# A half tile of 64 tokens paired on TensorE in a graph layer, and window values written to DRAM in 128-token tiles

## The chip, the cores and the metric

The kernel runs on one core of a Trainium2 chip. The metric is the device time of one execution in microseconds (us). TensorE is called PE, VectorE DVE, ScalarE ACT, GpSimd POOL; SP (SyncE) issues the DMAs.

## The reference

Four images of 56 x 56 positions (T = 3136 tokens) with 256 channels pass through four layers, all in fp32. Each layer adds its result to x, from a group norm of x:

- layer 0: attention of each token to its 7x7 neighbourhood, 8 heads;
- layer 1: a graph over all tokens of an image;
- layer 2: attention over neighbourhoods with dilation 1 and 2;
- layer 3: attention within shifted 7x7 windows of 49 tokens.

The change is in layers 1 and 3. Layer 1, cut to what matters:

```python
xn = x / norm(x, axis=-1)
A = exp(5.0 * (einsum('bnc,cc,bmc->bnm', xn, W_adj, xn) - max))
A = A * (1 - eye(n))
A = A / sum(A, -1)
diff = rowsum(A) * (x @ W_aff.T + b_aff) - (A @ x) @ W_aff.T
y = leaky_relu(layernorm(diff) * gamma + beta)
```

W_adj acts as a diagonal, so the matrix of exponentials is symmetric. Layer 3 is `softmax(q k^T * scale + bias + mask) v` for each window and head, followed by an output projection.

## The kernel before

**Layer 1** (L1331 to L1569). An image's tokens form NB = 25 tiles of 128, of which the last holds 64 tokens and is padded with zeros to 128. Chunks of four tiles are loaded by `tokens` (L1346): normalised, `xw` = x W_aff with a last column of -1 (257 columns), and `xnT`, the tokens at unit length with channels on the partitions. A block of exponentials is computed once for each pair of tiles j <= i and used for both, because the matrix is symmetric. The order of PE's work is that of a list of units (b, j, first, last): row tile j against up to four tiles from `first` to `last`. For each unit in turn:

- `transposed` (L1417) transposes its blocks, and ACT copies them to `at`;
- `logits` (L1404) of the *next* unit: two matmuls of up to 512 columns into `ps_s`, then ACT's exp into `e`; POOL clears the diagonal of a block with itself (L1414);
- `products` (L1429): for each tile i of the unit, `by_column` multiplies block e by xw of tile j into a PSUM bank `ps_v` (two banks, in turn), which DVE adds to `acc` of tile i (L1446; a copy for j = 0, L1444); `by_row` multiplies the transposed block by xw of tile i into `ps_o` of tile j (L1437).

When j has met all tiles, `finish` (L1465) forms and normalises its rows on DVE and POOL; its last step `add` (L1491 on) transposes the rows on PE (L1494) and adds them to x (L1502). Such small steps wait in a list and go out, when due, between the parts of a unit. `replace` (L1539) queues the chunks of the next image there as soon as the current image no longer needs their place, and `there` (L1533) runs what a unit's logits still lack.

**Values of layers 0 and 2.** `value_tiles` (L973) makes v = xn W_v in tiles of 128 tokens for a chunk of rows, in two pieces (a = 0, 1) of two tiles, adds the bias on DVE (L986), and after the second piece writes the whole to DRAM (`vd`, L991 and L993), from where it is gathered in the layout that attention needs (`vp`, L1688 in layer 2). A chunk's first tile begins with tokens left over from the chunk before (`left`, L969).

**Layer 3** (the code around L1837 to L1953). A row r is one of 32 rows of 8 windows, 392 tokens, handled as four window pairs of 98 tokens and in two halves of four heads (`hq`). `prepare` (L1859) normalises a row on DVE; `project_rows` (L1868) gives kT, qT and, by `value_rows` (L956), v for each window pair: 16 matmuls `ps_m<-w_wqkv,xn` with 98 rows of output and 256 columns (L962), evicted by DVE (L964). `quad` describes a half row for a shared attention routine: logits (L1025), exp and mask on ACT, DVE and POOL, products with v and with ones (L1040). The fill steps that PE does between logits and products are the output projection of row r-2 and the projections of row r+1 (L1929 to L1942). PE, DVE, ACT and POOL follow the written order in layer 3, PE does in layer 1; the rest, and SP's queue of DMAs throughout, is ordered by a scheduler at build time.

The functions that the change touches, with the line numbers of the profile:

Of the kernel before, what the change touches and what calls it, by code (L numbers as in the profile page):

```python
# [830 lines left out]
def direct_blocks(ctx: ExitStack, tc: tile.TileContext, d: dict, watch):  # L831
# [124 lines left out]
    def value_rows(v, a, n, xn, w, bias):  # L956

        pm = ps_m()
        for j in range(2):
            k = 2 * a + j  # L960
            for h in range(CC):
                nc.tensor.matmul(pm[:n, j * C:(j + 1) * C], lhsT=xn[:, h, k * n:(k + 1) * n],  # L962
                                 rhs=w[:, h, :], start=(h == 0), stop=(h == CC - 1))
        nc.vector.tensor_tensor(v[:, 2 * a:2 * a + 2, :], pm[:n, :].rearrange("p (j c) -> p j c", c=C),  # L964
                                bias[:n].rearrange("p (o c) -> p o c", o=1).to_broadcast([n, 2, C]), ALU.add)

# [6 lines left out]
    def value_tiles(v, a, c, n, xn, w, bias, dst):  # L973

        t0, t1 = c * n // P, (c + 1) * n // P if (c + 1) * n < T else -(-T // P)
        pm = ps_m()
        sizes = [min(P, T - t * P) for t in range(t0, t1)]
        mine = sizes[2 * a:2 * a + 2]
        for j, k in enumerate(mine):
            first = (2 * a + j) * P  # L980
            for h in range(CC):
                nc.tensor.matmul(pm[:k, j * C:(j + 1) * C], lhsT=xn[:, h, first:first + k], rhs=w[:, h, :],  # L982
                                 start=(h == 0), stop=(h == CC - 1))
        for k in sorted(set(mine)):
            js = [j for j, kj in enumerate(mine) if kj == k]
            nc.vector.tensor_tensor(  # L986
                v[:k, 2 * a + js[0]:2 * a + js[-1] + 1, :], pm[:k, js[0] * C:(js[-1] + 1) * C].rearrange("p (j c) -> p j c", c=C),
                bias[:k].rearrange("p (o c) -> p o c", o=1).to_broadcast([k, len(js), C]), ALU.add)
        if a == 1:
            whole = sizes.count(P)  # L990
            nc.sync.dma_start(out=dst[t0 * P:(t0 + whole) * P, :].rearrange("(k p) c -> p k c", p=P), in_=v[:, :whole, :])  # L991
            if whole < len(sizes):
                nc.sync.dma_start(out=dst[(t0 + whole) * P:T, :], in_=v[:sizes[-1], whole, :])  # L993
# [336 lines left out]

    def layer1(early, big, pool, brief):  # L1331
        NB = -(-T // P)
        real = lambda i: min(P, T - i * P)
# [4 lines left out]
        xnT = big.tile([P, CC, NB * P], FP, name="xnT")  # L1338
        xw = big.tile([P, NB, C + 1], FP, name="xw")
# [3 lines left out]
        nc.vector.memset(xw[T % P:, NB - 1, :], 0.0)  # L1343
        nc.vector.memset(xnT[:, :, T:], 0.0)

        def tokens(b, c, ps_a=ps_m):  # L1346

            tiles = range(4 * c, min(4 * c + 4, NB))
            n = sum(real(t) for t in tiles)
            k, m = real(tiles[0]), len(tiles)  # L1350
            box = {}

            def load():
                x = early.tile([P, CC, 512], FP, tag="x", name="x1")
                nc.sync.dma_start(out=x[:, :, :n], in_=tokens_of(1, b, 4 * c * P, n))
                x1 = box["x"] = early.tile([P, CC, 512], FP, tag="xn", name="xn1")
                sq = box["sq"] = early.tile([P, CC, 512], FP, tag="sq", name="sq", bufs=1)
                for h in range(CC):
                    normalise(x1[:, h, :n], x[:, h, :n], known(1, b), h)
                nc.scalar.activation(sq[:, :, :n], x1[:, :, :n], AF.Square)  # L1360
# [25 lines left out]
            def unit_length():  # L1386

                pm = ps_a()
                nc.tensor.matmul(pm[:, :n].rearrange("p (m k) -> p m k", k=k), lhsT=ones[:k, :], rhs=box["dg"][:k, :m, :k],
                                 start=True, stop=True)  # L1390
                nc.vector.tensor_tensor(xnT[:, :, 4 * c * P:4 * c * P + n], box["x"][:, :, :n],  # L1391
                                        pm[:, :n].rearrange("p (o k) -> p o k", o=1).to_broadcast([P, CC, n]), ALU.mult)

            return [load, lengths] + [lambda i=i: values(i) for i in range(0, m, 2)] + [unit_length]

        xd, out, xr = {}, {}, {}

# [6 lines left out]
        def logits(b, j, first, last):  # L1404

            n = (last - first) * P
            s = psum_tile("s", 2)
            for h in range(CC):
                nc.tensor.matmul(s[:, :n], lhsT=xd[j][:, h, :], rhs=xnT[:, h, first * P:last * P],  # L1409
                                 start=(h == 0), stop=(h == CC - 1))  # L1410
            e = pool.tile([P, 512], FP, tag="e", name="e1", bufs=3)
            nc.scalar.activation(e[:, :n], s[:, :n], AF.Exp, scale=5.0)  # L1412
            if first == j:
                nc.gpsimd.tensor_tensor(e[:, :P], e[:, :P], offd, ALU.mult)  # L1414
            return e

# [12 lines left out]
        def products(b, j, first, last, e, at):  # L1429
# [10 lines left out]
            def by_column(i):  # L1440
                pv = psum_tile("v", 2)
                nc.tensor.matmul(pv[:, :C + 1], lhsT=e[:, col(i)], rhs=xw[:, j, :], start=True, stop=True)  # L1442
                if j == 0:
                    nc.vector.tensor_copy(acc[:, i, :], pv[:, :C + 1])  # L1444
                else:
                    nc.vector.tensor_tensor(acc[:, i, :], acc[:, i, :], pv[:, :C + 1], ALU.add)  # L1446
# [10 lines left out]

        def residual(b, c):
# [6 lines left out]
        def finish(b, j):  # L1465

            n = real(j)
            y = pool.tile([P, C + 1], FP, tag="y", name="y", bufs=5)
# [3 lines left out]
            if j:  # L1472
                nc.vector.tensor_tensor(y[:n], out[j][:n, :C + 1], acc[:n, j, :], ALU.add)
            else:
                nc.vector.tensor_copy(y[:n], out[j][:n, :C + 1])
# [15 lines left out]
            def add():  # L1491
# [5 lines left out]
                while t0 < j * P + n:  # L1497
# [5 lines left out]
                    if t1 == (c + 1) * CH:  # L1503
# [7 lines left out]
        NC4 = -(-NB // 4)  # L1511
        units = [(b, j, i, min(i + 4, NB)) for b in range(NIMG) for j in range(NB) for i in range(j, NB, 4)]
        turn = iter(range(4 * NC4))
        fresh = [tokens(0, c, lambda: psum_tile(*(("v", 2), ("o", 2), ("t", 1), ("s", 2))[next(turn) % 4])) for c in range(NC4)]
        for c in range(2):
            fresh[c].pop(0)()
        for c in range(NC4):
            for step in fresh[c]:
                step()
            if c + 2 < NC4:  # L1520
                fresh[c + 2].pop(0)()
        scaled(0)
        e = logits(*units[0])
# [9 lines left out]
        def there(b, tile):  # L1533

            for item in [a for a in small if a[2] == (b, tile // 4)]:
# [3 lines left out]
        def replace(b, c):  # L1539
            load, *steps = tokens(b, c)  # L1540
            load()
            at = sum(a[2] is not None for a in small)
            small[at:at] = [(done + 8, step, (b, c)) for step in steps]

        for k, w in enumerate(units):
            b, j, first, last = w
            if first == j:
                residual(b, j * P // CH)
                residual(b, j * P // CH + 1)
                if b + 1 < NIMG and j % 4 == 2 and j >= 6:  # L1550
                    replace(b + 1, j // 4 - 1)
                if b + 1 < NIMG and j == NB - 1:
                    replace(b + 1, NC4 - 2)
                if b and j == 0:
                    replace(b, NC4 - 1)
            small_step()
            at = transposed(*w, e)
            if k + 2 < len(units) and units[k + 2][1] == units[k + 2][2]:
                scaled(units[k + 2][1])
            if k + 1 < len(units):  # L1560
                there(units[k + 1][0], units[k + 1][3] - 1)
                ahead = logits(*units[k + 1])
            small_step()
            products(*w, e, at)
            done += last - first
            if last == NB:
                small.append((done + 6, finish(b, j), None))
# [260 lines left out]
    def layer3(early, big, pool, brief):  # L1828
# [10 lines left out]
        xs, xns, qkv, attns = {}, {}, {}, {}  # L1839
# [19 lines left out]
        def prepare(r):  # L1859
# [3 lines left out]
            xn = xns[r] = early.tile([P, CC, WC], FP, tag="xn", name="xn3")  # L1863
            for h in range(CC):
                for w, xv in parts(xn[:, h, :], x[:, h, :]):
                    normalise(w, xv, known(3, r // 8), h)

        def project_rows(r):  # L1868
            xn = xns.pop(r)
            qT = pool.tile([P, CC, WC], FP, tag="q", name="q3")  # L1870
            kT = pool.tile([P, CC, WC], FP, tag="k", name="k3")
            v = pool.tile([98, 4, C], FP, tag="v", name="v3")
            qkv[r] = qT, kT, v
# [9 lines left out]
            def values(a):  # L1883
                value_rows(v, a, 98, xn, w_qkv[:, :, 2 * C:], bv3)

            return [lambda f=f, m=m: f(m) for m in range(2) for f in (keys, queries, values)]

        def quad(r, hq):
            b, wr = divmod(r, 8)
            qT, kT, v = qkv[r]  # L1890
# [14 lines left out]
            def piece(u):  # L1905
                sl = slice(u * 98, (u + 1) * 98)
                return (lambda j: kT[hr(j), hq, sl], lambda j: qT[hr(j), hq, sl],
                        lambda j: v[:, u, (4 * hq + j) * HD:(4 * hq + j + 1) * HD], True, True)
# [20 lines left out]
        def stream():  # L1929
            n = NIMG * 8  # L1930
            for r in range(n):
                attns[r] = pool.tile([P, CC, WC], FP, tag="attn", name="attn3", bufs=3)
                rows = lazily(project_rows, r + 1, 6) if r + 1 < n else []
                out = project_out(r - 2) if r > 1 else []
                for hq in range(CC):
                    steps = out[hq:hq + 1] + rows[3 * hq:3 * hq + 3]
                    if hq and r + 2 < n:
                        steps.append(lambda r=r: prepare(r + 2))
# [6 lines left out]
        prepare(1)  # L1945
        for step in project_rows(0):
            step()
        attend_quads(pool, stream())
# [117 lines left out]
```

## Time and profile before

| what | value |
|---|---|
| median of 3 runs | 4103.79 us (4103.39 to 4105.45) |
| the profiled execution, its own time | 4092.52 us |
| its span, first to last instruction | 4090.7 us |
| mean granted PE clock | 0.979 of full |
| layer 1 | about 809 to 2839 us of the span |
| layer 3 | about 3540 us to the end |
| column products L1442 | 2400 records, 666.6 us busy |
| row products L1437 | 2400 + 200 records, 663.2 + 60.7 us busy |
| logits L1409 | 1456 records, 622.9 us busy |
| transposes L1423 | 1200 records, 192.0 us busy |
| additions to `acc` on DVE L1446 | 1104, 421 ns each |
| layer 3's value matmuls L962 | 512 records, 121.3 us busy |
| their evictions on DVE L964 | 64, 692 ns each |

How to read it: busy times of PE are modelled to the end of each matmul and overlap their successors, so a matmul's price is better read from the distance between starts. An fp32 matmul leaves two records, a transpose one. A timeline line gives the start and duration of a group in us, its line, the tiles out<-in, the tile of the array that it uses (rows*columns), its shape and the number of records.

### The profile page before, as it was taken

How to read it: one execution, taken by the hardware profiler on the slowest of the kernel's cores; microseconds unless marked ns; L12 is line 12 of the kernel's file. 1: busy time of each engine (PE TensorE's matmuls, PEld its weight loads, DVE VectorE, ACT ScalarE, POOL GpSimd, SP SyncE). 2: the span in 40 equal slices, each digit the busy share in tenths (PEclk: the TensorE clock that was granted, in tenths of full speed). 3: DMA queues.
4: the chain of work that ended last, by engine and by line, in shares of the span. 5: the costliest groups of instructions: out<-in, count | busy, mean ns of one | idle time of the engine just before them, and what ended most of it. 6: DMA issues, size and time to landing. Idle time of an engine off the chain costs nothing. (4 is left out here: it accounts for less than half of the span.)

```text
span 4090.7 us, 92322 instructions
## 1 busy us (share of the span) xinstructions
PE 3889.7 (95%) x39031; PEld 2778.1 (68%) x39031; DVE 2369.5 (58%) x4445; ACT 1377.7 (34%) x2890; POOL 1741.9 (43%) x1883
## 2 busy tenths in 40 slices
PE   7899999899999999999999999997999999999998
PEld 4566666577777677776777767775676766666665
DVE  6777777634445444454344543444688877666665
ACT  3445555322222122222222212222555555444443
POOL 2576767621123211242112421123677777554544
PEclk9899999899999999999999999998999999999999
DMA  7344333210000100001000000002344443322221
GB/s 259 101 136 126 116 116 104 90 32 10 15 15 24 34 10 15 15 24 34 10 15 15 23 23 9 10 19 108 108 135 124 131 118 111 108 72 73 73 75 63
DMA packets 239986, 275.88 MB, mean 67 GB/s; under 512 B 22342, under 2 KB 231912, under 8 KB 239080
## 3 DMA queue, kind: packets, MB, share of 16 engines
q1 hardware_dynamic: 239274, 269.80, 21.0%
q8 instruction: 309, 5.06, 0.5%
q14 instruction: 115, 0.94, 0.1%
q10 hardware_dynamic: 288, 0.08, 0.0%
HBM read 190.29 MB, written 79.53 MB: 66 GB/s over the span
## 5 line engine op out<-in xcount | busy, mean ns | idle before, releaser
L1446 DVE TENSOR_TENSOR acc<-acc,ps_v 128x257 f32<-128x257 f32 x1104 | 457.7, 421 | 679.2 <-PE ps_v L1442 676.5
L1442 PE MATMUL ps_v<-xw,e 128*128 128x257 f32 x2400 | 666.6, 382 | 27.2 <-DVE acc L1446 17.2
L1437 PE MATMUL ps_o<-xw,at 128*128 128x257 f32 x2400 | 663.2, 380 | 0.0
L1409 PE MATMUL ps_s<-xnT,xd 128*128 128x512 f32 (+3 forms) x1456 | 622.9, 550 | 5.1 <-DVE xnT L1391 5.1
L1442 PEld LDWEIGHTS ps_v<-xw,e 128*128 128x128 f32 x2400 | 445.0, 189 | 193.2 <-issue 91.8
L1426 ACT COPY at<-ps_t 128x512 f32<-128x512 f32 (+3 forms) x360 | 184.8, 513 | 1053.7 <-PE ps_t L1423 1053.7
L1091 POOL TENSOR_TENSOR b<-e 126x336 f32<-126x336 f32 (+5 forms) x512 | 499.7, 997 | 11.6 <-ACT e L1079 3.6
L1437 PEld LDWEIGHTS ps_o<-xw,at 128*128 128x128 f32 x2400 | 455.9, 190 | 65.5
L1402 POOL TENSOR_SCALAR xd<-xnT,vec 128x128 f32<-128x128 f32 x200 | 122.2, 622 | 707.4 <-PE ps_s L1409 705.6
L945 PE MATMUL ps_m<-xn,w_wqkv 128*128 128x392 f32 x1024 | 380.1, 505 | 2.7 <-DVE xr L1729 2.7
L1082 POOL TENSOR_TENSOR e<-e,m0t 126x672 f32<-126x672 f32 (+3 forms) x128 | 239.3, 1870 | 271.1 <-ACT e L1081 229.6
L1409 PEld LDWEIGHTS ps_s<-xnT,xd 128*128 128x128 f32 x1456 | 245.1, 191 | 155.6 <-issue 138.8
L1082 POOL TENSOR_TENSOR e<-e,bias 119x784 f32<-119x784 f32 (+5 forms) x128 | 244.6, 1911 | 202.0 <-ACT e L1081 200.8
L1412 ACT ACTIVATE e<-ps_s 128x512 f32<-128x512 f32 (+3 forms) x364 | 200.8, 552 | 376.7 <-PE ps_s L1409 376.0
L1003 ACT ACTIVATE no<-rs 128x168 f32<-128x168 f32 (+2 forms) x256 | 93.8, 367 | 596.2 <-DVE rs L1694 271.7
L945 PEld LDWEIGHTS ps_m<-xn,w_wqkv 128*128 128x128 f32 x1024 | 189.4, 192 | 126.1 <-ACT pr L1922 17.5
L1100 PEld LDWEIGHTS ps_o<-e,vp 124*32 124x32 f32 (+3 forms) x8192 | 176.9, 111 | 142.3 <-issue 94.8
L1100 PE MATMUL ps_o<-e,vp 124*32 124x112 f32 (+3 forms) x8192 | 239.5, 254 | 6.1 <-POOL e L1082 4.5
L939 DVE TENSOR_SCALAR xn<-x,gst 128x28 f32<-128x28 f32 (+5 forms) x368 | 206.1, 614 | 56.4 <-PE ps_m L945 27.7
L1079 ACT ACTIVATE e<-e 126x672 f32<-126x672 f32 (+5 forms) x256 | 219.5, 857 | 19.2 <-DVE e L1078 6.2
L1694 DVE RECIPROCAL rs<-ps_o 128x196 f32<-128x196 f32 (+2 forms) x128 | 176.0, 1375 | 78.8 <-PE ps_o L1100 78.3
L1032 POOL TENSOR_TENSOR e<-e,m3l 98x784 f32<-98x784 f32 x64 | 118.2, 1847 | 236.1 <-ACT e L1029 236.1
(169 smaller groups left out, 6176.6 us busy)
## 6 DMA issues: line engine op xcount, KB each, us to landing
x<-xr SPq DMA_DIRECT2D x64, 392.0 KB
x<-in_x SPq DMA_DIRECT2D x53, 448.0 KB
xr<-x SPq DMA_DIRECT2D x60, 392.0 KB
x<-x SPq DMA_DIRECT2D x60, 392.0 KB
vd<-v SPq DMA_DIRECT2D x48, 384.0 KB
xr<-in_x SPq DMA_DIRECT2D x32, 392.0 KB
xr<-x SPq DMA_DIRECT2D x28, 448.0 KB
x<-xr SPq DMA_DIRECT2D x28, 448.0 KB
```

Source lines behind the costliest of these rows:

```text
L939: nc.vector.tensor_scalar(dst, src, gst[:, h, 0:1], gst[:, h, 1:2], ALU.subtract, ALU.mult)
L945: nc.tensor.matmul(pm[:, :n], lhsT=w[:, h, col:col + P], rhs=rhs(h), start=(h == 0), stop=(h == CC - 1))
L1079: nc.scalar.activation(ev, ev, AF.Exp)
L1082: nc.gpsimd.tensor_tensor(parts(ev), parts(ev), w["emask"], ALU.mult)
L1091: nc.gpsimd.tensor_tensor(w["b"][a][:nk, :, :2 * nq].rearrange("p h (i c) -> p h i c", i=2), ev[:, :, :, 0, :], ev[:, :, :, 1, :], ALU.add)
L1100: nc.tensor.matmul(w["o"](k, i)[j * HD:(j + 1) * HD], lhsT=ones[:nk, :HD] if k else v(j, u), rhs=w["b"][j // 2][:nk, j % 2, i * nq:(i + 1) ...
L1409: nc.tensor.matmul(s[:, :n], lhsT=xd[j][:, h, :], rhs=xnT[:, h, first * P:last * P], start=(h == 0), stop=(h == CC - 1))
L1412: nc.scalar.activation(e[:, :n], s[:, :n], AF.Exp, scale=5.0)
L1426: nc.scalar.copy(at[:, sl], pt[:, sl])
L1437: nc.tensor.matmul(out[j][:, :C + 1], lhsT=e[:, col(i)] if i == j else at[:, col(i)], rhs=xw[:, i, :], start=(i == j), stop=(i == NB - 1))
L1442: nc.tensor.matmul(pv[:, :C + 1], lhsT=e[:, col(i)], rhs=xw[:, j, :], start=True, stop=True)
L1446: nc.vector.tensor_tensor(acc[:, i, :], acc[:, i, :], pv[:, :C + 1], ALU.add)
```

## The change

Layer 1:

- NB becomes 24 full tiles; the 64 remaining tokens (REST) are handled apart. Their tile is loaded twice, side by side, so that one copy lies on partitions 0 to 63 and one on 64 to 127 of `xw`.
- The half tile is the row side of its blocks now, not the column side: three rest units of an image (q = 0, 1, 2) take eight full tiles each. `rest_logits` makes [64, 512] logits for four tiles on the upper half of the partitions and for four on the lower half (a = 0, 1). `rest_transposed` transposes the stacked block once for both. `rest_products` makes, for each i, a pair of products with 64 rows of contraction into two `ps_v` banks and a pair with 64 rows of output into the halves of `ps_o`. The half tile's own block of 64 x 64 goes into the third unit.
- The results of the three rest units are added up in `racc`, and `finish` of the half tile is started after the third of them; its `add` goes out after j = 23.
- Rest units q = 0, 1 of an image are placed after j = 20 and 21 of the image before (for the first image ahead of all), q = 2 after j = 0. As q = 0, 1 come first, they copy to `acc` (a = 0 on DVE, a = 1 on ACT) and the later units add.
- `replace` is called at other places (j = 3, 6, 10, 14, 18, 20, 22), and runs first what is pending of the chunk before.

Layers 0, 2 and 3: `value_tiles` issues a DMA for each evicted piece.

Layer 3: `value_rows` is gone. Values come from `value_tiles` in tiles of 128 tokens, for row r+2, as the last fill step of a half row; they go to DRAM (`vd3`), and `gather` fetches row r+1 from there as [98, 4, 256]. `xn` gets 448 columns, the first of which are the left-over tokens of the row before, copied by ACT; `prepare` runs one row further ahead (three `xn` buffers). The prologue makes the values of two rows ahead of the projections of row 0.

Instructions before and after: `ps_v` products 1200 full / 1104 full and 96 half; `ps_o` 1300 full / 1200 full and 96 half, with 4 own blocks; transposes 1200 / 1152; logits of 512 columns 576 / 528 and 48 half; layer 3's value matmuls 256 / 200; DMAs issued by SP 1601 / 1765. In SP's order the loads of layer 3's `w_qkv` and of its rows 0 and 1, which stood in layer 1 and in the middle of layer 2 (2402, 2966 and 2987 us), come at the end of layer 2.

The diff, cut to its core:

```diff
@@ value_tiles
-        if a == 1:
-            whole = sizes.count(P)
-            nc.sync.dma_start(out=dst[t0 * P:(t0 + whole) * P, :].rearrange("(k p) c -> p k c", p=P), in_=v[:, :whole, :])
-            if whole < len(sizes):
-                nc.sync.dma_start(out=dst[(t0 + whole) * P:T, :], in_=v[:sizes[-1], whole, :])
+            t = t0 + 2 * a + js[0]
+            nc.sync.dma_start(out=dst[t * P:min((t + len(js)) * P, T), :].rearrange("(k p) c -> p k c", p=k),
+                              in_=v[:k, 2 * a + js[0]:2 * a + js[-1] + 1, :])
@@ layer1
+        def add_up(b, i, pv, copy=nc.vector.tensor_copy):
+            if (b, i) in touched:
+                nc.vector.tensor_tensor(acc[:, i, :], acc[:, i, :], pv[:, :C + 1], ALU.add)
+            else:
+                touched.add((b, i))
+                copy(acc[:, i, :], pv[:, :C + 1])
+        def rest_logits(q):
+            s = psum_tile("s", 2)
+            for a in range(2):
+                for h in range(CC):
+                    nc.tensor.matmul(s[a * REST:(a + 1) * REST, :], lhsT=xdr[:, h, a * REST:(a + 1) * REST],
+                                     rhs=xnT[:, h, (2 * q + a) * 512:(2 * q + a + 1) * 512], start=(h == 0), stop=(h == CC - 1))
+            e = pool.tile([P, 512], FP, tag="e", name="e1", bufs=3)
+            nc.scalar.activation(e, s, AF.Exp, scale=5.0)
...
+        def rest_products(b, q, e, own, at):
+            po = psum_tile("o", 2)
+            for i in range(4):
+                pv = [psum_tile("v", 2) for a in range(2)]
+                for a in range(2):
+                    half = slice(a * REST, (a + 1) * REST)
+                    nc.tensor.matmul(pv[a][:, :C + 1], lhsT=e[half, i * P:(i + 1) * P], rhs=xw[half, NB, :], start=True, stop=True)
+                for a in range(2):
+                    add_up(b, 8 * q + 4 * a + i, pv[a], (nc.vector.tensor_copy, nc.scalar.copy)[a])
+                for a in range(2):
+                    nc.tensor.matmul(po[a * REST:(a + 1) * REST, :C + 1], lhsT=at[:, i * P + a * REST:i * P + (a + 1) * REST],
+                                     rhs=xw[:, 8 * q + 4 * a + i, :], start=(i == 0), stop=(i == 3 and (a == 1 or own is None)))
+            if own is not None:
+                nc.tensor.matmul(po[:REST, :C + 1], lhsT=own, rhs=xw[:REST, NB, :], start=False, stop=True)
+            if q == 0:
+                nc.vector.tensor_copy(racc, po[:, :C + 1])
+            else:
+                nc.vector.tensor_tensor(racc, racc, po[:, :C + 1], ALU.add)
...
+                if j == 0:
+                    units.append((b, None, 2))
+                if b + 1 < NIMG and 0 <= j - 20 < 2:
+                    units.append((b + 1, None, j - 20))
...
+                if j in (3, 6, 10, 14, 18, 20, 22):
+                    replace(b + 1, {3: NC4, 20: 4, 22: 5}.get(j, j // 4 - 1))
@@ layer3
+            c = r % 8
+            xn = xns[r] = early.tile([P, CC, 448], FP, tag="xn", name="xn3", bufs=3)
+            at = left(c, WC)
...
+            if at:
+                end = left(c - 1, WC) + WC
+                nc.scalar.copy(xn[:, :, :at], ahead[0][:, :, end - at:end])
...
+        def gather(r):
+            b, c = divmod(r, 8)
+            vs[r] = pool.tile([98, 4, C], FP, tag="v", name="v3")
+            nc.sync.dma_start(out=vs[r], in_=vd[b][c * WC:(c + 1) * WC, :].rearrange("(k p) c -> p k c", p=98))
+        def values(r):
+            b, c = divmod(r, 8)
+            xn = xns[r]
+            v = pool.tile([P, 4, C], FP, tag="vt", name="vt3", bufs=1)
+            def step(a):
+                value_tiles(v, a, c, WC, xn, w_qkv[:, :, 2 * C:], bv3, vd[b])
+                if a == 0 and r:
+                    gather(r - 1)
+                if a and r == NIMG * 8 - 1:
+                    gather(r)
...
-                    steps = out[hq:hq + 1] + rows[3 * hq:3 * hq + 3]
-                    if hq and r + 2 < n:
-                        steps.append(lambda r=r: prepare(r + 2))
+                    steps = out[hq:hq + 1] + rows[2 * hq:2 * hq + 2] + ahead_values[hq:hq + 1]
+                    if hq and r + 3 < n:
+                        steps.append(lambda r=r: prepare(r + 3))
```

## The prediction

> **What bounds the kernel now.** I read the page first: totals, slices, chain. PE works 95% of the span, nothing else passes 58%, and PE leads the chain that ended last. So PE time counts.
>
> ```profile
> span 4090.7 us, 92322 instructions
> PE 3889.7 (95%) x39031; PEld 2778.1 (68%) x39031; DVE 2369.5 (58%) x4445; ACT 1377.7 (34%) x2890; POOL 1741.9 (43%) x1883
> PE 37%; DVE 3%; POOL 1%; DMA 1%; issue 1%; ACT 0%; SPq 0%; POOLq 0%; DVEq 0%; ACTq 0%
> ```
>
> Then the windows, to see if that holds where the edit is. Layer 1 is 809 to 2839 us, layer 3 follows 3540. Columns: window, its length, then each engine's busy time.
>
> ```profile
> 850.00:1350.00 500.00, 489.29 (x2141) 364.65 (x2140) 216.13 (x568) 103.95 (x194) 118.35 (x186) 0.99 0.05 17
> 2350.00:2860.00 510.00, 479.64 (x2090) 354.29 (x2088) 221.97 (x599) 106.35 (x197) 119.04 (x190) 0.98 0.09 32
> 3540.00:4091.00 551.00, 531.12 (x7426) 361.70 (x7425) 354.36 (x514) 218.86 (x384) 263.32 (x322) 0.99 0.22 70
> ```
>
> In layer 1 PE is busy 489 of 500 us, DVE 216; in layer 3, 531 of 551, DVE 354. Hence PE prices come from distances between starts in PE's timeline. First a layer 1 unit (start, duration, count of records; an fp32 matmul is two records, a transpose one):
>
> ```profile
> 1506.58 0.60 PE L1423 MATMUL ps_t<-ident,e 128*128 128x128 f32 x4
> 1507.01 1.88 PE L1409 MATMUL ps_s<-xnT,xd 128*128 128x512 f32 x4
> 1508.73 1.03 PE L1442 MATMUL ps_v<-xw,e 128*128 128x257 f32 x4
> 1509.60 0.60 PE L1437 MATMUL ps_o<-xw,at 128*128 128x257 f32 x2
> ...
> 1512.20 0.60 PE L1423 MATMUL ps_t<-ident,e 128*128 128x128 f32 x4
> ```
>
> Four transposes take 0.43 us (0.109 each), a 512-column matmul 1.72/2 = 0.857, a 257-column one 0.433. The next unit follows with no gap.
>
> **Layer 1, what goes.** Tile 24 holds 64 tokens padded to 128. Taken out over the four images: 96 column products and 100 row products (196 × 0.433 = 84.9 us), 48 transposes (5.2), 48 matmuls of 512 columns net (41.1), 8 of 128 columns (1.7), old small-tile switches in the ending (3.2). Sum 136.1.
>
> **Layer 1, what comes.** 48 pairs of row-half products (64x128 tiles), 48 pairs of column-half products (128x64), 24 pairs of logits, 4 own blocks. Nothing in layer 1 runs small tiles side by side now; layer 3 does:
>
> ```profile
> 3600.31 0.95 PE L1025 MATMUL ps_s<-q,k 32*98 32x98 f32 x32
> 3601.19 1.58 PE L945 MATMUL ps_m<-attn,w_wp 128*128 128x392 f32 x4
> ...
> 3605.24 1.89 PE L962 MATMUL ps_m<-w_wqkv,xn 128*98 128x256 f32 x8
> 3607.06 0.89 PE L1040 MATMUL ps_o<-e,v 98*32 98x98 f32 x32
> ...
> 3608.55 0.95 PE L1025 MATMUL ps_s<-q,k 32*98 32x98 f32 x32
> ```
>
> 32 records of 98 columns in 0.88 us: one after the other, at the 0.84 ns a column of layer 1, they need 2.6, so four run together, row-tiled (L1025) and column-tiled (L1040). A pair of halves is two instructions on two tiles, so I price it as one: 96 × 0.433 = 41.6. The bound on the other side is no overlap, 83.1.
>
> The logits pairs are issued first half h0, h1, then second half h0, h1. If starts keep program order, the second half's h0 starts beside the first half's h1, and a unit takes 3 × 0.857 = 2.57; free overlap is 1.71, none 3.43. Here the row decides nothing: layer 3 changes tile with every instruction. The Trainium skill does ("TensorE: Matmul & The Clock Gate", Part 3: Packing small matmuls: matmuls start and end in program order), against "up to 2×" in "TensorEngine Tiling (Array Packing)", Theoretical Speedup. By the first 12 × 2.57 = 30.9, by the second 20.6. I take 30.9. Own blocks 2.6 (estimate: 8 short records plus switches).
>
> **The price of changing tile shape.** Layer 2 has it: eight 256-column records, of which the last four (merged into the row) are of the 64-token tile:
>
> ```profile
> 358.38 2.14 PE L982 MATMUL ps_m<-w_wv,xn 128*128 128x256 f32 x8
> 360.45 0.38 PE L921 MATMUL ps_m<-dv,group 128*128 128x2 f32 x2
> ```
>
> 2.07 us from start to start, where 8 × 0.216 = 1.73: one switch in and one out cost 0.34. Record by record it is a 0.093 drain each, plus the weight load that is then uncovered, 0.05 for 64 columns, 0.107 for 128: 0.146 in, 0.200 out. The skill's tiling page (Key Properties: switching mode drains TensorE) gives no price; counting pairs alone would put the change at zero for this. A rest unit alternates row pair, column pair four times, and its logits stand between full units: four to column form (0.58), four to row form (0.80), one out (0.20), logits in and out (0.35) = 1.93; × 12 = 23.2, and 0.6 around the own blocks.
>
> Added: 41.6 + 30.9 + 2.6 + 23.8 = 98.9. Layer 1's PE: −37.2.
>
> **Layer 1's waits.** The rows' spacing covers about 1947 of layer 1's 2030 us. What shows of the rest are short units at an image's end:
>
> ```profile
> PE ps_v L1442 <- DVE acc L1446: 17.2, 23, 1.7
> PE ps_m L1494 <- DVE xr L1502: 5.7, 1, 5.7
> ```
>
> (Total, times, longest.) Some 12 us an image are such stalls over 0.2 us, and the layer's last stores stand 13 us after its last product. Between j = 20 and j = 22 the new order puts four-pair units of the next image, with DVE and ACT sharing the first copies, and the half tile's `finish` is long done at the end. I take −11. Bounds: 0 (every stall moves on to the new last tile) and −20. Against it: in the q = 2 units both banks are emptied by DVE, 2 × 0.42 us against the column pair's 0.58 + 0.20 cover; some 0.25 us × 3 × 4 = 3; behind the waiting row pair stand the column pair and the next transposes, for which ACT waits. Net −8. The extra steps (`racc` on DVE, first copies on ACT, `xdr` on POOL, four more loads on SP) lie on engines busy 43%, 21%, 24% there, and on an SP that issues 34 us in the layer: nothing, but for the DVE queue just priced. `replace` now runs leftover steps of the chunk before at once; the same instructions, cover DVE's 57% idle time; without cover a `unit_length` is some 1 us of DVE.
>
> **Layer 3.** Value matmuls fall from 256 to 25 tiles × 2 × 4 = 200; one costs 1.82/4 = 0.455 including switch (5.24 to 7.06), 0.431 alone. 56 × 0.431 = −24.1. The pace has no room for another owner: from L1025 to L1025 8.24 us, PE without gaps; the shorter units keep it, since the exp ends on POOL at 3612.5 and PE wants it at 3615.3. DVE evictions shrink (692 ns twice a row to about 680 + 413, from layer 2's rows); the ACT copy of left-over columns, about 0.5 us a row, is on an engine busy 40%.
>
> The values now go through DRAM: 68 writes, 32 gathers at 0.4 to 0.7 us of SP (layer 2's issues). SP issues only 43 us in layer 3, but it is in order: a gather waits for its write's landing, and behind it wait the store and the loads. From the eviction of row r+2 to the first use of row r+1's values are two units, 16.5 us. The chain needs 0.7 (eviction) + 0.45 + 3.7 (the longest wait for a written `vd` in layer 2) + 0.7 + 3.7 (taken alike) = 9.3. Slack 7 us, cost nothing. A store issued later by that is covered too: SP now waits 377 us in layer 3 for POOL's residual.
>
> The start of layer 3 costs: in SP's new order the weights and rows 0 and 1, loaded long before now, come behind layer 2's last gathers and stores (near 3519 to 3534 us), so `prepare` falls to the boundary, where PE already waits 2.7 us. I take +7 (2: only the load of one row shows; 12: load, normalise and values in series).
>
> **Layers 0 and 2.** Values are written in two pieces: 60 more writes at 0.45 us on SP, which issues 73% of the time in layer 2. First pieces leave earlier. I take 0, bounds ±8.
>
> **Sum.** −37.2 − 8 − 24.1 + 7 = −62.3 on the span of 4090.7: 4028.4. The profiled execution ran 1.8 above its span, the median 13.1 above it: 4041.5.
>
> **Rivals.**
> - *Logits overlap freely*: −10.3 more, 4031. For it: the four-tile rows; against it: program order. 18%.
> - *Most stalls of layer 1 vanish too*: 20 instead of 8, and the boundary hidden: 4022. 13%.
> - *Pairs don't overlap*: +20.8 twice and +10.3, 4093. Against it stand L1025 and L1040; for it, that no two-tile form is in the trace. 9%.
> - *SP or new waits in rest units take 24*: 4065. 5%.
> - *Slower, the late gather*: a gather later than the 7 us of slack stops PE at L1040 in each row, and with it the next logits behind it, for which DVE, ACT and POOL wait. 2 us beyond (write and gather landing in 16.6 together, not 7.4) eats 31 × 2 = 62, all the gain; from 2.3 us it is slower by over 0.2%, and 4 us beyond give 4165. For it: SP's order and the 1 KB packets; against it: 0.22 DMA share. 3%.
>
> My forecast holds 52%, own range 4030 to 4052. That the change does not do what it says is excluded: the instruction lists show the counts above.
>
> **Chances.** Some 0.2% (8 us) is what a measurement here can tell from none. The first four cases and the fifth but for half of no overlap are faster: 0.94; same 0.03, slower 0.03. Range 4014 to 4066: it leaves out no overlap, the late gather and tails.
>
> **What would show it.** Right: ps_v and ps_o pairs starting a few ns apart, 0.2 us holes at each change of shape, a rest logits group of 2.6 us, layer 1 near 1985 us, layer 3 units alternately near 8.2 and 7.4 us, no PE wait on `v3`. Wrong: pairs of 0.87 us, waits of PE on DVE inside rest units, PE idle before L1040, or over 10 us lost at the start of layer 3 or in layer 2.

## The result, and the profile after

The changed kernel takes 4058.47 us (median of 4 runs, 4050.30 to 4062.50), the kernel before 4104.62 beside it (4 runs, 4103.39 to 4109.14): a ratio of 0.9885, 95% interval 0.9869 to 0.9901, or −46 us. In a later set of runs (f0 below) the ratio was 0.9903 (0.9882 to 0.9924). The forecast was 4041, −62: right in sign and within its range, about 17 us too hopeful.

The page of the profiled execution after (4059.2 us):

```profile
span 4057.4 us, 92345 instructions
PE 3849.6 (95%) x38871; PEld 2718.7 (67%) x38871; DVE 2356.9 (58%) x4431; ACT 1379.5 (34%) x2922; POOL 1747.1 (43%) x1883
```

PE is still busy 95% of the span: the kernel is bound as before, with less PE work. To see where the time went I cut both traces at the same instructions:

| stretch | before | after | difference |
|---|---|---|---|
| layer 0, to layer 1's first matmul | 809.1 | 813.8 | +4.7 |
| layer 1, to its first logits | 40.3 | 43.2 | +2.9 |
| layer 1, first logits to last transpose of its result | 1989.0 | 1965.9 | −23.1 |
| layer 2 | 697.0 | 695.3 | −1.7 |
| layer 3 with its start | 555.2 | 539.1 | −16.1 |
| span | 4090.7 | 4057.4 | −33.3 |

The two profiled executions differ by 33, the medians by 46: the profiled one of before lay 12 below its median. Later runs of before reach from 4085 to 4106, so a few us of any single trace mean nothing. What layer 3 was to bring (−17) is nearly there: −16 in this pair, −12 to −16 in the seven other traces with the same layer 3. What layer 1 was to bring (−45) is half missing.

For layer 1's main stretch I split PE's time: for each record, the distance to the next start against the pace of its columns (0.833 ns a column and 2.2 ns). What is over stands at a change of tile shape, or is a wait that the trace shows, or is a record that ran slower than its pace. All in us:

| layer 1, main stretch | pace of the work | waits | at changes of shape | slower than pace | rest |
|---|---|---|---|---|---|
| before | 1902.5 | 51.5 | 3.1 | 24.4 | 7.5 |
| after | 1841.5 | 55.6 | 23.5 | 37.6 | 7.7 |
| e4, first copies on ACT | 1844.8 | 43.9 | 20.1 | 32.2 | 7.7 |
| f1, rest units inside rows, chunks earlier | 1840.0 | 49.1 | 13.4 | 33.7 | 7.8 |

The work fell by 61. The two columns of switching and slowness together rose by 33.6, and the waits rose by 4 where they should have fallen by 8. PE's waits in that stretch (total, times, longest):

```profile
PE ps_v L1495 <- DVE acc L1418: 18.1, 25, 1.5
PE ps_v L1457 <- DVE acc L1421: 11.1, 8, 1.6
...
PE ps_v L1457 <- DVE acc L1418: 8.5, 8, 2.1
```

L1495 is the full column product, and its wait is that of before (17.2, 23 times). L1457 is the rest unit's row pair: 19.6 us of waiting for DVE, none of which existed before. Here is one such unit (q = 2 of the second image) on PE, then DVE over the same time:

```profile
1410.37 0.70 PE L1457 MATMUL ps_v<-xw,e 64*128 64x257 f32 x4
1411.00 0.65 PE L1461 MATMUL ps_o<-xw,at 128*64 128x257 f32 x4
1411.82 0.70 PE L1457 MATMUL ps_v<-xw,e 64*128 64x257 f32 x2 [0.17 <-DVE acc L1418]
1414.60 1.23 PE L1457 MATMUL ps_v<-xw,e 64*128 64x257 f32 x2 [2.08 <-DVE acc L1418]
1415.76 1.13 PE L1461 MATMUL ps_o<-xw,at 128*64 128x257 f32 x4
```

```profile
1410.95 0.41 DVE L1539 TENSOR_SCALAR y<-y,mv,rstd 128x256 f32<-128x256 f32 x1 [0.68 <-POOL rstd L1538]
...
1411.35 0.42 DVE L1418 TENSOR_TENSOR acc<-acc,ps_v 128x257 f32<-128x257 f32 x1
1413.56 0.66 DVE L1542 SCALAR_TENSOR_TENSOR y<-y 128x256 f32<-128x256 f32 x1 [1.79 <-POOL y L1541]
1414.14 0.74 DVE L1418 TENSOR_TENSOR acc<-acc,ps_v 128x257 f32<-128x257 f32 x2
```

DVE adds one bank at 1411.35, then stands 1.79 us for POOL in the last step of the row's `finish`; the second bank's addition is queued behind that step. PE waits 2.08 us for a bank whose emptying takes 0.42. It is the same in each of the ten rest units that wait: DVE stands 1.3 to 2.1 us for POOL in a `finish` ahead of the eviction, and in the three q = 1 units a chunk's `xnT` step of 1.21 us (L1384) stands between the two as well. The second reading is in the last two PE lines: the row pair takes 1.23 instead of 0.70, the column pair 1.13 instead of 0.65. The windows (last columns: granted PE clock, DMA share, GB/s) give this unit, and a stretch with the first image's rest units, whose products wait for nothing:

```profile
1410.00:1422.00 12.00, 9.75 (x40) 3.98 (x40) 4.50 (x14) 0.60 (x1) 3.40 (x6) 0.72 0.00 0
860.00:876.00 16.00, 15.31 (x85) 6.10 (x82) 4.02 (x13) 5.58 (x12) 1.39 (x3) 0.96 0.02 8
```

The granted clock is 0.72 in the one, 0.96 in the other. So a wait can be paid twice here: the trace's clock is at full or at half, and over the main stretch PE worked at half clock for 53 us, 15 before. At half pace, half of that is lost, so the 38 more come to some 19 us (an estimate from these two numbers).

The rest logits, in the timeline:

```profile
1322.97 1.94 PE L1428 MATMUL ps_s<-xnT,xdr 128*64 128x512 f32 x8
1324.85 0.70 PE L1490 MATMUL ps_o<-xw,e 128*128 128x257 f32 x2
```

1.88 us from start to start, a switch included: two times 0.857, not three. Layer 3's start and two of its half rows:

```profile
3515.62 2.47 PE L945 MATMUL ps_m<-attn,w_wp 128*128 128x392 f32 x7
3522.74 7.52 PE L971 MATMUL ps_m<-w_wqkv,xn 128*128 128x256 f32 x24 [4.66 <-DVE xr L1802]
3533.68 7.22 PE L945 MATMUL ps_m<-xn,w_wqkv 128*128 128x392 f32 x16 [3.42 <-DVE vt L975]
```

```profile
3700.63 0.95 PE L1012 MATMUL ps_s<-q,k 32*98 32x98 f32 x32
...
3705.57 1.03 PE L971 MATMUL ps_m<-w_wqkv,xn 128*128 128x256 f32 x4
...
3708.02 0.95 PE L1012 MATMUL ps_s<-q,k 32*98 32x98 f32 x32
...
3712.95 1.89 PE L971 MATMUL ps_m<-w_wqkv,xn 128*128 128x256 f32 x8
...
3716.27 0.95 PE L1012 MATMUL ps_s<-q,k 32*98 32x98 f32 x32
```

PE waits 8.1 us at the start (2.7 before), and the 24 value records between them take about 0.31 us apiece instead of 0.216. The half rows are 7.39 and 8.25 us, with values for one tile and for two, and nothing waits for `v`.

### The profile page after: what moved, and what is told of

Same layout as the page of the kernel before. It is cut to its first block, busy times and chain, and to the rows that moved or that the text cites. A ratio compares the mean times of both kernels' runs of the same rounds, so it can differ in the third digit from the quotient of the medians.

```text
span 4057.4 us, 92345 instructions
## 1 busy us (share of the span) xinstructions
PE 3849.6 (95%) x38871; PEld 2718.7 (67%) x38871; DVE 2356.9 (58%) x4431; ACT 1379.5 (34%) x2922; POOL 1747.1 (43%) x1883
## 4 chain that ended last, share of the span: by engine, by line
PE 48%; DVE 3%; POOL 2%; DMA 1%; issue 1%; SPq 0%; ACT 0%; DVEq 0%; POOLq 0%; ACTq 0%
PE ps_m L945 12%; PE ps_o L1490 6%; PE ps_s L1406 6%; PE ps_v L1495 6%; PE ps_m L971 4%; PE ps_o L1087 3%; PE ps_s L1058 3%; PE ps_o L1027 2%; PE ps_t L1476 1%; PE ps_s L1012 1%; PE ps_m L1374 1%; DMA x<-x 0%; DVE rs L1767 0%; PE ps_m L1361 0%; PE ps_v L1457 0%
## 5 line engine op out<-in xcount | busy, mean ns | idle before, releaser
L1495 PE MATMUL ps_v<-xw,e 128*128 128x257 f32 x2208 | 613.2, 382 | 20.2 <-DVE acc L1418 18.1
L1490 PE MATMUL ps_o<-xw,at 128*128 128x257 f32 x2208 | 609.0, 379 | 0.0
L1406 PE MATMUL ps_s<-xnT,xd 128*128 128x512 f32 (+3 forms) x1344 | 571.1, 547 | 0.0
L1495 PEld LDWEIGHTS ps_v<-xw,e 128*128 128x128 f32 x2208 | 408.6, 189 | 171.6 <-issue 80.4
L1479 ACT COPY at<-ps_t 128x512 f32<-128x512 f32 (+3 forms) x332 | 170.4, 513 | 997.2 <-PE ps_t L1476 997.0
L1490 PEld LDWEIGHTS ps_o<-xw,at 128*128 128x128 f32 x2208 | 419.2, 190 | 60.0
L1406 PEld LDWEIGHTS ps_s<-xnT,xd 128*128 128x128 f32 x1344 | 225.5, 191 | 134.8 <-issue 126.2
L1409 ACT ACTIVATE e<-ps_s 128x512 f32<-128x512 f32 x336 | 185.5, 552 | 332.8 <-PE ps_s L1406 332.8
L945 PEld LDWEIGHTS ps_m<-xn,w_wqkv 128*128 128x128 f32 x1024 | 189.5, 191 | 126.3 <-ACT pr L2019 17.2
L939 DVE TENSOR_SCALAR xn<-x,gst 128x28 f32<-128x28 f32 (+4 forms) x368 | 203.8, 608 | 50.2 <-PE ps_m L945 28.4
L971 PE MATMUL ps_m<-w_wqkv,xn 128*128 128x256 f32 (+1 forms) x800 | 207.4, 398 | 18.2 <-DMA w_wqkv<-in_wqkv 8.5
```

What stands on the lines that cost most here:

```text
L939: nc.vector.tensor_scalar(dst, src, gst[:, h, 0:1], gst[:, h, 1:2], ALU.subtract, ALU.mult)
L945: nc.tensor.matmul(pm[:, :n], lhsT=w[:, h, col:col + P], rhs=rhs(h), start=(h == 0), stop=(h == CC - 1))
L1490: nc.tensor.matmul(out[j][:, :C + 1], lhsT=e[:, col(i)] if i == j else at[:, col(i)], rhs=xw[:, i, :], start=(i == j), stop=(i == NB - 1))
```

## The experiments

My theory A: layer 1's missing gain is PE waiting for evictions that stand in DVE's queue behind a `finish` that waits for POOL, and the lower clock after such waits. Rivals: the split value writes of layers 0 and 2 cost it (B), the clock belongs to the run (C), two PSUM banks are too few for pairs anywhere (D).

**e1 and e2: each half of the change alone.** e1 has the new layer 1 and the old values, e2 the reverse:

```text
  e1:  layer1 as changed;  value_rows, value_tiles, layer 3 as before
  e2:  layer1 as before;   value_tiles, layer 3 as changed
```

> Layer 1 as changed; the values of layers 0, 2 and 3 as before. Theory A (the half tile's rest units lose about 20 us to PE waiting for DVE's evictions, and some 10 more to a slower PE clock behind those waits; all else came as summed): layer 1 shortens by about 20 to 28, the rest stays, so about 4080, 20 to 28 below before. Rival B (the split value writes of layers 0 and 2 ate the missing gain): layer 1 alone brings 38 or more, 4066 or less. Rival C (the slower PE clock belongs to the run, not to the rest units): 30 to 40 below before.

> Layer 1 as before; the values in 128-token tiles through DRAM in layer 3, and the split writes in layers 0 and 2, as changed. Theory A: layer 3 with its start shortens by 16 to 18, layers 0 and 2 stay within 4, so about 4087. Rival B: layers 0 and 2 lose 10 or more, so 4094 or above. Rival C says nothing of this one beyond the theory.

Measured: e1 4069.65 against 4095.13 of before, ratio 0.9940 (0.9922 to 0.9957), −25; e2 4080.90, ratio 0.9960 (0.9946 to 0.9974), −14 by the medians. In e1's trace layer 1 is 23 shorter, layer 3 the same as before. In e2 layers 0 and 2 are within 2 us of before, layer 3 with its start 543.6 instead of 555.2. The two ratios add up to the whole. B falls: without the split writes layer 1 brings no more. Layer 0 took 804 to 814 us in all traces with split writes and 806 to 809 in the two without; its +4.7 is no cost that can be told from the spread.

**e3: rest units inside rows.**

```diff
-                if j == 0:
-                    units.append((b, None, 2))
-                if b + 1 < NIMG and 0 <= j - 20 < 2:
-                    units.append((b + 1, None, j - 20))
+                    if (j, i) == (0, 12):
+                        units.append((b, None, 2))
+                    if b + 1 < NIMG and (j, i) in ((13, 17), (19, 19)):
+                        units.append((b + 1, None, int(j == 19)))
```

> The changed kernel with the rest units placed inside a row (after the units that begin at tile 12 in row 0, 17 in row 13, 19 in row 19) and so not right behind a row's finish chain on DVE. Theory A: PE's wait for DVE in rest units falls from 19.6 to below 7 us, the slow records go with it, 15 to 25 below the changed kernel, about 4038. Rival C: the waits move or go, but the clock stays: within 8 of the changed kernel. Rival D (two banks are too few for pairs, wherever they stand): waits of about 20 stay, no change.

Measured: 4057.96, ratio 0.9907 (0.9892 to 0.9921): no better than the changed kernel, and my number was wrong by 20. Yet the wait that the theory spoke of had gone. What PE waited for in layer 1:

```profile
PE ps_m L1382 <- DVE xw L952: 6.6, 9, 0.9
PE ps_m L1374 <- DVE rn L1363: 5.6, 3, 1.9
...
PE ps_m L1374 <- ACT xw L954: 4.1, 6, 0.7
PE ps_m L1547 <- DVE xnT L1384: 3.9, 3, 1.3
...
PE ps_v L1457 <- DVE acc L1421: 0.6, 3, 0.2
```

Rest units wait 0.6 us instead of 19.6, against D. In its place stand 20 us of waits at L1374, L1382 and L1547, the steps of chunks of the next image: a rest unit needs its two chunks whole, and with q = 1 moved from row 21 to row 19, one row after its chunk is loaded, all its steps are made at once, each waiting for the eviction of the one before. A second loss stands in no list of waits, because PE is at work while it happens:

```profile
1318.95 3.31 PE L1428 MATMUL ps_s<-xnT,xdr 128*64 128x512 f32 x8
1322.19 0.70 PE L1490 MATMUL ps_o<-xw,e 128*128 128x257 f32 x2
```

These rest logits take 3.24 us at full clock, where they took 1.88: their second half waits for DVE's `xnT` step of the chunk made just ahead, and the first half has run alone by then. It is so in six of the twelve groups, 7 to 8 us together. So waits had been changed for others. Nor did the lower clock go with the rest units' waits, as A had said: PE worked at half clock for 41 us of the stretch, now behind other waits. The number of rival C (within 8 of the changed kernel) is the one that came, and f1 has to decide.

**e4: first copies on ACT.**

```diff
-                    add_up(b, 8 * q + 4 * a + i, pv[a], (nc.vector.tensor_copy, nc.scalar.copy)[a])
+                    add_up(b, 8 * q + 4 * a + i, pv[a], nc.scalar.copy)
```

> The changed kernel with the first copies of both halves on ACT (before: one on DVE, one on ACT); the units that add (q = 2) still need DVE. Theory A: the 11 us of waits for DVE's first copies go, the 8.5 us in the q = 2 units stay, with the clock 10 to 16 below the changed kernel, about 4045. Rival D: two copies in a row on ACT take 0.74 us for a cover of 0.78, so the waits move to ACT: within 4 of the changed kernel.

Measured: 4039.49, ratio 0.9854 (0.9835 to 0.9872), 15 to 19 below the changed kernel. In the trace:

```profile
PE ps_v L1495 <- DVE acc L1418: 18.0, 25, 1.5
...
PE ps_v L1457 <- DVE acc L1418: 8.5, 8, 2.1
```

The 11.1 us for DVE's copies are gone, the 8.5 of the q = 2 units stay, as A has it. ACT needs 0.37 us for a copy and has nothing of `finish` in its queue: what counted was not the time of a copy but whose queue it stood in. Layer 1's main stretch is 17 shorter: 11.7 of waits and 8.8 of slowness and switches, 3.3 given back in the work's pace: with both copies on one engine the second bank comes free later, and every second row pair took 0.84 us instead of 0.63 (this much is true of D). The lower clock did not need a wait in front of it:

```profile
1337.65 3.13 PE L1428 MATMUL ps_s<-xnT,xdr 128*64 128x512 f32 x8
```

```profile
1337.00:1341.00 4.00, 4.00 (x12) 1.40 (x13) 0.16 (x1) 1.42 (x3) 2.06 (x2) 0.61 0.00 0
```

These logits come behind a q = 0 unit and 2 us of one-column matmuls, and no wait of PE over 0.15 us stands in the 14 us ahead of them; yet the clock was at half for 3.4 us. e4 has three such stretches.

**f0: the changed kernel again, f1: inside rows with earlier chunks.** f1 places q = 0 and 1 as e3 does, puts q = 2 behind the unit that begins at tile 10 of row 2, and loads chunks 2 and 3 at rows 13 and 16 (its other edit is that of e3 with (2, 10) for (0, 12)):

```diff
-                if j in (3, 6, 10, 14, 18, 20, 22):
-                    replace(b + 1, {3: NC4, 20: 4, 22: 5}.get(j, j // 4 - 1))
+                if j in (3, 6, 10, 13, 16, 20, 22):
+                    replace(b + 1, {3: NC4, 6: 0, 10: 1, 13: 2, 16: 3, 20: 4, 22: 5}[j])
```

> The changed kernel as it is, beside the others on one chip, as their yardstick. All theories: 4050 to 4062, PE waits for DVE in rest units about 19.6 us, layer 1's logits to last transpose 1966 us.

> Rest units inside rows again (after tile 10 of row 2, tile 17 of row 13, tile 19 of row 19), and now the chunks that they need are replaced two or three rows earlier, so that no step of a chunk has to be made in a hurry. Theory A (the eviction queue on DVE behind a finish chain is the loss, and hurried chunk steps were what replaced it in the first placing inside rows): waits in rest units below 2 us, hurried chunk steps below 5, layer 1's main part 1938 to 1948 where the changed kernel has 1966, total 18 to 28 below the changed kernel. Rival D (any place costs the same): 1966 again, within 6.

Measured: f0 4054.95, waits in rest units 19.7 us and layer 1's main stretch 1962.9; f1 4035.22, ratio 0.9850 (0.9832 to 0.9868), 20 below f0, main stretch 1944.2. A rest unit of f1:

```profile
1812.83 0.70 PE L1457 MATMUL ps_v<-xw,e 64*128 64x257 f32 x4
1813.46 0.65 PE L1461 MATMUL ps_o<-xw,at 128*64 128x257 f32 x4
1814.04 0.70 PE L1457 MATMUL ps_v<-xw,e 64*128 64x257 f32 x4
...
1817.12 0.65 PE L1461 MATMUL ps_o<-xw,at 128*64 128x257 f32 x4
1817.70 0.44 PE L1547 MATMUL ps_m<-ident,y 128*128 128x128 f32 x2
```

4.87 us for its products, where the sum of the prediction has 8 × 0.433 + 1.38 = 4.85 (its switches but the one into it); the unit shown above took 10.8 to its own block. The granted clock of 1811 to 1819 us is 1.00. Chunk steps still wait 15 us in f1 (I had said under 5), so the total waits fall only from 55.6 to 49.1; the larger part of the gain is in the switches and slowness, 61.1 to 47.1. Against e3, whose main stretch was 1970.3, f1 is 26 shorter with only 5 us less of chunk waits: its rest logits run in halves side by side again, and its clock is better. PE worked at half clock for 21 us of the main stretch in f1 (21 again in f2, 29 in g2), 48 in f0 and 53 in the changed kernel's first trace. That answers C: the lower clock goes with where the rest units stand, not with the run. That the waits alone bring it down is not shown; e4 speaks against it.

**f2: `finish` in parts.**

```diff
-            nc.vector.tensor_scalar(y, y, mv[:n, 0:1], rstd[:n], ALU.subtract, ALU.mult)
-            nc.gpsimd.tensor_tensor(y, y, gamma[:n], ALU.mult)
-            nc.gpsimd.tensor_tensor(y, y, beta[:n], ALU.add)
-            nc.vector.scalar_tensor_tensor(y, y, 0.01, y, ALU.mult, ALU.max)
+            def norm():
...
+            def leaky():
...
+                    small += [(done + 1 + 2 * i, f, None) for i, f in enumerate(parts)]
```

> As the kernel with rest units inside rows and earlier chunks, and the finish of a row is given out in three parts, so that DVE does not stand waiting for POOL with evictions behind it. Theory A: the 18 us of waits of full column products for additions to acc fall to below 9, 8 to 15 below the kernel before it. Rival E (DVE's own work in the short rows at an image's end is the bound, not its wait for POOL): those 18 us stay, no difference over 4.

Measured: 4033.67, ratio 0.9847 (0.9829 to 0.9865), no different from f1. The waits at L1495 are 21.3 us (25 times), not 9. My expectation failed: giving out the steps in parts is not enough. Whether DVE's own work in the short rows is the bound (E), or where the scheduler puts the parts on DVE, this run does not separate.

**f3 and g3: the start of layer 3.** f3 has two `xn` buffers instead of three; with them the built order loads the weights in layer 1 again. g3 has two `vt` buffers as well:

```diff
-            xn = xns[r] = early.tile([P, CC, 448], FP, tag="xn", name="xn3", bufs=3)
+            xn = xns[r] = early.tile([P, CC, 448], FP, tag="xn", name="xn3")
-            v = pool.tile([P, 4, C], FP, tag="vt", name="vt3", bufs=1)
+            v = pool.tile([P, 4, C], FP, tag="vt", name="vt3")
```

> The changed kernel with two instead of three xn buffers in layer 3, which by the built order brings the weights' load back to where it stood before the change, in layer 1. Theory F (the late loads at the start of layer 3 cost their idle time and a slow clock after it, 8 to 12 us together): 6 to 12 below the changed kernel, PE idle at that boundary near 2.7. Rival G (three buffers are needed: DVE's normalise waits for the projections that read the buffer): layer 3 gets longer by 5 or more, PE waits for values or keys inside rows.

> The changed kernel with two xn and two vt buffers in layer 3, nothing else. Theory F, sharpened (the wait of 3.2 us for vt before the projections of row 0 is the second row's eviction waiting for the first row's write from the single vt buffer): that wait goes, PE idle at the start falls from 8 to about 3, layer 3 with its start from 540 to 533, total 6 to 9 below the changed kernel. Rival J (the wait is for something else, the row's x or its normalise): within 3 of the kernel with two xn buffers alone, 4052.

Measured: f3 4051.67 (0.9893, 0.9872 to 0.9914), 3 below f0, which is within the spread and short of the 6 that theory F asked for: PE still waited 6.5 us at the start; g3 4047.54 (0.9874, 0.9853 to 0.9894). By the traces layer 3 with its start took 540.6 us in f0, 536.9 in f3, 534.6 in g3. The wait for `vt` in g3 is gone:

```profile
3512.56 8.02 PE L971 MATMUL ps_m<-w_wqkv,xn 128*128 128x256 f32 x24 [3.86 <-DVE xr L1802]
3520.49 5.53 PE L945 MATMUL ps_m<-xn,w_wqkv 128*128 128x392 f32 x16
```

So that wait was the single `vt` buffer, whose second row's eviction had to let the first row's write land. G falls: no wait in rows came with two `xn` buffers. What is left, 3.9 us for layer 2's last residual, is near the 2.7 of before. Against f0 the medians differ by 7, with intervals that overlap.

**g1: the order of the logits halves.**

```diff
-            for a in range(2):
-                for h in range(CC):
+            for h in range(CC):
+                for a in range(2):
```

> The changed kernel with the rest units' logits issued half by half in turn (first product of both halves, then second of both) instead of one half and then the other. Theory H (matmuls on two tiles run independently, so a later instruction on a free tile starts ahead of an earlier one that waits for its own tile): the group takes 1.71 us plus switches in either order, no change, but the two halves' starts lie 7 rather than 13 ns apart. Rival I (the build had already paired them and starts keep program order): the same 1.71, and the same 13 ns.

Measured: 4055.31 (a single run). At full clock the groups take 1.868 us to the next start (1.874 in the changed kernel), and the halves' records start 6 to 7 ns apart instead of 13. In the program of the changed kernel both products of the first half stand ahead of the second half's, so the second half's first product overtakes the first half's second. H holds. e3's trace shows it by line numbers: two records of the own block (L1436), which the program has behind the rest logits (L1428), start at 1390.03 us, ahead of three of these.

**g2: f1 with the two buffer counts.**

> Rest units inside rows with earlier chunks, and in layer 3 two xn buffers and two vt buffers. Theory F with A: the gain of the first (20 below the changed kernel) and of the start of layer 3 (4 to 10) add up: 4023 to 4032. Rival: the two overlap or the start gives nothing: 4035.

Measured: 4032.49, ratio 0.9840 (0.9823 to 0.9858), −64 against before. It is the lowest ratio of the study, and below the changed kernel beyond doubt; against f1 (4035.22) the difference is within the spread. Layer 3 with its start is shorter than f1's (535.9 against 542.9), layer 2 longer (697.7 against 691.5); whether the earlier loads cause the latter is open.

## Why the prediction was right, and where it was off

- *The work.* Removed and added matmuls measured −61 in layer 1 and −24 in layer 3 (pace 500.0 to 476.1), forecast −58 and −24.1 without switches. With the logits' 10 (below) layer 1 should have shown −68. Part of what is missing stands where the halves of a pair did not start together, because the second bank came free later: 30 of the 192 row-half records, 16 in f1.
- *Pairs run as one*: right, starts 7 ns apart, and a clean unit takes the sum's 4.87.
- *The price of switching*: right. In f1, where waits do not blur it, switches and slowness are 19.6 us above before, some 3 of them the clock's; 23.8 − 3.2 = 20.6 had been put there.
- *Logits in program order, 30.9*: wrong. The rival at 18% was true; 1.88 us a group with its switch at full clock, so 20.6 of pace in all (two of the twelve ran at half clock and took 3.3 and 3.6). This gave 10 us back, so the sum's error elsewhere is larger than it looks: that the total came within 17 us is in part luck, two errors of opposite sign.
- *Layer 1's waits, −8*: this is the term that failed; +4 came. I priced DVE's time (two additions against 0.78 us of cover, 3 us in the q = 2 units) and wrote that the other additions to busy queues cost nothing. The trace shows 8.5 us in the q = 2 units and 11.1 in the others, in ten of the twelve rest units, because these ten come right behind a row's last unit, whose `finish` holds DVE for POOL. The forecast had named such waits as a sign of its being wrong. The other half of the term was right: the old stalls fell from 51.5 to 36, by 15, where 11 had been taken.
- *The clock*: not in the sum at all. About 14 us in layer 1 (61.1 in the two columns, less the 47.1 of f1), 16 by the time at half clock (half of 53 − 21), and some 5 in layer 3, where records slower than pace rose from 13.2 to 18.2.
- *Layer 3's start, +7*: 5.4 of waiting, with the clock about 10. Right in mechanism for the late loads, but half of the wait was a buffer that I had not looked at.
- *The gather and SP*: no PE wait for `v3`, as forecast; the slower rival did not happen.
- *Layers 0 and 2*: 0, as far as the runs can tell.

In the traces: −41 for layer 1's work with switches, +4 and +14 for waits and clock, +3 ahead of its first logits, −16 for layer 3 and +3 for the rest make the −33 of the profiled pair. How much of the difference between that and −46 is the run that happened to be profiled cannot be said; the repeated ratio stands at −40.

## What to carry to other kernels

When work is moved onto an engine that is half idle, price the place in its queue, not its busy share: look at what the instruction ahead of it waits for. A wait of the bounding engine can cost more than its length, so add the pace of what follows to the wait. And when a wait has been taken away, read the waits again before believing the gain: in e3 it had moved to other lines, and a part of it to records that ran alone, which no list of waits shows.

## What the runs showed of the hardware

- After PE waits of 1.6 to 2.1 us in rest units, the clock was at half for 3.4 or 6.8 us, once for 13.7 (granted clock 0.72 in the window above), and so it was for the first value records after the 4.66 us at layer 3's start: 0.427 us apart, then 0.216. The Trainium skill ("TensorE: Matmul & The Clock Gate", Part 1: The HAM clock gate) lets the clock fall after an idle window of about 3.4 us; here shorter waits between small-tile groups were followed by it, though not all: the unit at 913 us waited 1.6 and kept its pace. In e4 the clock fell three times behind a rest unit and some one-column matmuls with no wait over 0.15 us in the 14 us ahead. What brings it down stays open.
- Matmuls on different tiles of the array are not held to program order: the same page's Part 3 has starts in program order, while here a later instruction on a free tile ran ahead of an earlier one on its own busy tile, and issue order made no difference (1.874 and 1.868 us).
- A change of tile shape cost 0.15 to 0.20 us in layer 1 as it did in layer 2: in f1's unit a row pair takes 0.63 us to the next start and a column pair 0.58, where 0.433 is the pace. Of this, 0.09 stands at the change itself, and 0.10 or 0.05 between the two records of a pair.
